# First attention: the causal triangle selected in SBUF by GpSimd, late exponentials, and products three steps behind the scores

## The chip, the cores and the metric

The kernel runs on one NeuronCore of one Trainium2 chip, in one launch. The metric is the device time in microseconds, as the median of several executions. A core has five engines that work side by side, each through its own queue in order: TensorE (PE), VectorE (DVE), ScalarE (ACT), GpSimd (POOL), and SyncE (SP), which here only issues transfers. They wait for each other through semaphores.

## The reference

The reference is a block of four parts over x of 1024 tokens by 512 channels: an attention of 32 heads of 16 channels, a mixture of low-rank experts, a second attention of 32 heads of 128 channels, and the experts again. The change lies in the first attention alone:

```python
x = x + _L0_attn_a_ref(_layernorm(x, axis=-1), wq, wk, wv, wo)

# inside, with hd = 16
scores = jnp.einsum('bqhd,bkhd->bhqk', xq, xk) * scale
causal = jnp.tril(jnp.ones((T, T), dtype=bool))
scores = jnp.where(causal[None, None], scores, NEG_INF)
probs = jax.nn.softmax(scores, axis=-1)
out = jnp.einsum('bhqk,bkhd->bqhd', probs, xv).reshape(B, T, C)
return out @ wo.T
```

Token q may only look at tokens k up to q. Everything is float32.

## The kernel before

`attention_a` first projects (`project_a`), then attends (`attend_a`). The 32 heads, each padded to 32 rows, make eight *chunks* `c` of four heads. Every chunk is computed twice over: once with queries on the partitions (*rows*, `row_scores` L358) to find each query's maximum, and once with keys on the partitions (*columns*, `col_scores` L407), where the maximum has been put into a spare channel of q, so that the scores come out with the maximum already taken off. The exponentials of the columns (`exponentials` L429) are then directly the left side of the product with v (`product` L449). One spare column of v holds ones, so the product also gives the sums of the softmax.

A chunk is cut into nine *steps* `n`, lists of pieces that make up to 512 score columns a head. In chunks 0 to 6 the columns go through `down_cols`: steps 0 to 3 are full blocks, step 4 is the diagonal of the second half of the queries (`qc` 1), 5 is beside it, 6 holds its rest and the first piece of `qc` 0, 7 is the diagonal of `qc` 0, and 8 its rest. Chunk 7 goes through `up_cols`, which begins with the diagonal of `qc` 0.

`step(rc, cc, n)` (L534) works on the rows of chunk `rc = cc + 1` and the columns of chunk `cc` at once, in two halves of two heads each. A half records: four score tiles on PE (two of columns, two of rows, each in a PSUM bank of `ps_s`, which has seven), the maxima on DVE (`maxima` L375, L378), the two exponentials on ACT, then whatever is due, then half of the product of an earlier step. `pending` holds the steps whose product is still to come; before the change a step's product is recorded two steps later (`len(pending) > 2`, L541).

In the diagonal steps 4 and 7, `exponentials` has the triangle added on PE: for each head four bfloat16 matmuls with the identity `identb` and `maskT` (L427) add -2^100 above the diagonal to the scores that are already in the bank, and the exponential then gives zero there.

`later` is a list of recorded work with a count; `due()` (L526) runs once in each half, lowers every count and records what has fallen below zero. It carries the end of a chunk. When the last product of a (chunk, qc) is recorded, `normalize` (L482) copies the sums and results out of the one PSUM bank of `ps_o` on ACT (L486), has SP move them (L493, L495), and puts two pieces into `later`: `invert` after 3 halves (the reciprocal L498 on DVE, transfers L500 and four of L502 that spread the inverses into `over`), and `multiply` after 8 (L508 on POOL, which needs the transfers of L495 and L502). Before the change `normalize` of `qc` 1 is reached in the first half of step 8 of its own chunk, and that of `qc` 0 in the second half of step 1 of the next. For chunks 6 and 7 `normalize_turned` (L468) does this with transposes on DVE. `with_maxima` (L389) transposes the maxima of the next chunk and has SP write them into q by four transfers (L397), at the end of steps 6 and 8.

The order in which instructions stand in each engine's queue is not that of the recording: a scheduler in the Tile layer orders them by its own estimate of when each could run. Instructions given to `keep_in_program_order` (the reciprocal L498 among them) keep their recorded order on their engine. Semaphore waits follow from what each instruction reads and writes. The tiles `p` of the exponentials come from the pool `a_pt` with five buffers of four heads by 512.

## Time and profile before

| what | value |
|---|---|
| median of 3 runs | 1570.44 us (1569.54 to 1571.32) |
| the profiled execution | 1571.58 us, its span 1569.8 us |
| busy share of the span: PE, DVE, ACT, POOL | 98%, 67%, 42%, 29% |
| mean granted PE clock | 0.999 |
| exponentials of the columns (L429) | 292 of 0.417 to 0.680 us, from 120.6 to 370.4 us |
| mask matmuls (L427) | 256 of 0.38 us, from 132.3 to 365.1 us |
| product matmuls (L449) | 1552, from 125.5 to 371.2 us |
| copies out of PSUM (L486) | 12 of 0.593 us, from 148.7 to 322.0 us |
| reciprocals (L498) | 12 of 0.533 us, from 155.9 to 329.2 us |
| multiplies on POOL (L508) | 12 of 1.272 us, from 165.2 to 338.7 us |

The span is the time from the first to the last instruction of one profiled execution; the execution's own time is 1.8 us longer. A row of a group gives the line, engine, operation, what it writes and reads, its shape and count, then its busy time in us and the mean in ns of one, and last the idle time of the engine just before such instructions and what ended it ("<-"). A row of a timeline gives the start, the length, the engine ("SPq" is SP's queue of transfers, whose length is that of issuing), the line and what ran, with the idle time before it and its releaser in brackets. Several instructions that follow each other without a gap are drawn as one row with their number, so a row of 1.08 us with "x2" is a pair of exponentials. A row of a stretch gives its bounds, its length, the busy time and number of instructions of PE, weight loads, DVE, ACT and POOL, the granted clock of PE as a share of the full one, and the share and rate of the transfers. A matmul's end is modelled, so a busy PE is not one at its peak.

### The profile page before, as it was taken

To read this page: it belongs to the slowest core of one execution; us is meant where nothing else is said; L and a number is where in the kernel's file an instruction comes from. 1 tells how busy PE (TensorE), PEld (TensorE's weight loads), DVE (VectorE), ACT (ScalarE), POOL (GpSimd) and SP (SyncE) were. 2 spreads that over 40 slices of the span, in tenths; PEclk is the share of its full clock that TensorE was granted. 3 is DMA by queue.
4 is the path that set the end of the run, shared out by engine and by line. 5 is a ranking of instruction groups with operands and counts; after the bars stand their busy time and mean duration, and the time that the engine had idled before them with its cause. 6 is when DMAs were issued, how large, how long until landed. Compare 5 with 4: busy or idle time off the path is not lost.

```text
span 1569.8 us, 32216 instructions
## 1 busy us (share of the span) xinstructions
PE 1543.4 (98%) x12894; PEld 926.1 (59%) x12894; DVE 1058.7 (67%) x2537; ACT 662.1 (42%) x1597; POOL 463.1 (29%) x571
## 2 busy tenths in 40 slices
PE   9999999999999999999999999999999999999998
PEld 5545455555555657557656755755765675556654
DVE  4557778773566886666776667766676766776753
ACT  2216666665223544443434444343343444433430
POOL 3000000002233433432443343334244333333450
PEclk9999999999999999999999999999999999999999
DMA  5000222220033102412330331241133032135001
GB/s 208 1 1 6 20 22 19 18 20 19 29 99 95 42 1 68 68 42 55 63 60 28 82 38 31 65 72 41 54 62 61 28 69 35 34 86 122 4 2 54
DMA packets 80950, 75.34 MB, mean 48 GB/s; under 512 B 14944, under 2 KB 56672, under 8 KB 80800
## 3 DMA queue, kind: packets, MB, share of 16 engines
q1 hardware_dynamic: 70272, 52.56, 14.3%
q0 software_dynamic: 8848, 17.58, 7.7%
q10 hardware_dynamic: 1680, 3.15, 0.5%
q8 instruction: 101, 1.65, 0.5%
q14 instruction: 49, 0.40, 0.1%
HBM read 33.08 MB, written 18.87 MB: 33 GB/s over the span
## 4 chain that ended last, share of the span: by engine, by line
PE 84%; DVE 7%; POOL 4%; ACT 2%; issue 2%; SPq 0%; DMA 0%; DVEq 0%; ACTq 0%; POOLq 0%
PE s L1079 13%; PE wo L765 12%; PE o L1140 11%; PE sT L407 8%; PE pq L993 8%; PE kv L920 5%; PE oT L449 5%; PE pm_f L714 3%; PE or L1140 3%; PE s L358 3%; PE pj_v L218 2%; PE pj_q L218 2%; PE pm_ao L1370 2%; PE pj_k L218 2%; DVE p L1081 2%
## 5 line engine op out<-in xcount | busy, mean ns | idle before, releaser
L1091 POOL TENSOR_SCALAR p<-p,rs 128x1024 f32<-128x1024 f32 (+7 forms) x256 | 192.8, 754 | 407.0 <-DVE rs L1090 406.3
L1079 PE MATMUL s<-kT,qT 128*128 128x512 f32 (+3 forms) x768 | 297.0, 496 | 10.9 <-DVE p L1081 10.9
L1079 PEld LDWEIGHTS s<-kT,qT 128*128 128x128 f32 x768 | 137.9, 190 | 174.7 <-issue 114.4
L765 PE MATMUL wo<-wo,oT 128*128 128x512 f32 x512 | 237.9, 593 | 1.0 <-ACT spare L781 1.0
L1106 DVE STREAM_TRANSPOSE pT<-p 128x512 f32<-128x512 f32 (+3 forms) x256 | 152.9, 602 | 109.5 <-PE o L1140 58.8
L1088 ACT ACTIVATE p<-p,nm 128x1024 f32<-128x1024 f32 (+7 forms) x256 | 198.3, 775 | 17.9 <-ACT nm L1086 0.4
L429 ACT ACTIVATE p<-sT 128x512 f32<-128x512 f32 (+1 forms) x292 | 155.2, 593 | 89.8 <-PE s L358 35.2
L1085 DVE TENSOR_REDUCE nm<-p 128x1 f32<-128x1024 f32 (+7 forms) x256 | 188.2, 735 | 2.9
L1140 PEld LDWEIGHTS o<-pT,va 32*128 32x128 f32 x4212 | 172.9, 185 | 21.7 <-issue 10.4
L1086 ACT ACTIVATE nm<-nm 128x1 f32<-128x1 f32 x256 | 51.6, 202 | 315.6 <-DVE nm L1085 314.7
L1140 PE MATMUL o<-pT,va 32*128 32x224 f32 (+5 forms) x4212 | 181.3, 324 | 0.8 <-DVE pT L1106 0.8
L358 PE MATMUL s<-kT,qT 32*128 32x512 f32 (+3 forms) x768 | 164.4, 520 | 0.0
L407 PE MATMUL sT<-qT,kT 32*128 32x128 f32 (+3 forms) x1152 | 155.3, 401 | 0.3 <-DMA qT<-negT 0.3
L765 PEld LDWEIGHTS wo<-wo,oT 128*128 128x128 f32 x512 | 94.2, 190 | 90.7 <-issue 78.8
L1081 DVE SCALAR_TENSOR_TENSOR p<-s,rq,relr 128x512 f32<-128x512 f32 x192 | 120.9, 646 | 9.9 <-PE s L1079 9.7
L993 PE MATMUL pq<-xnTb,wq 128*128 128x512 f32 x240 | 117.8, 600 | 0.4
L1081 DVE SCALAR_TENSOR_TENSOR p<-s,rq,rel 128x512 f32<-128x512 f32 (+1 forms) x192 | 102.5, 558 | 21.0 <-PE s L1079 20.9
L407 PEld LDWEIGHTS sT<-qT,kT 32*128 32x128 f32 x1152 | 80.6, 184 | 50.6 <-issue 29.4
L1112 DVE STREAM_TRANSPOSE tT<-p 128x512 f32<-128x512 f32 (+3 forms) x128 | 63.7, 498 | 57.0 <-POOL p L1091 30.6
L375 DVE TENSOR_REDUCE part<-s 128x1 f32<-128x512 f32 x128 | 81.6, 684 | 28.1 <-PE s L358 20.1
L1090 DVE RECIPROCAL rs<-ss 128x1 f32<-128x1 f32 x256 | 39.8, 155 | 85.9 <-ACT p L1088 82.1
L508 POOL TENSOR_TENSOR o<-o,over 64x512 f32<-64x512 f32 x12 | 15.3, 1272 | 270.1 <-DMA o<-oTs 224.0
(201 smaller groups left out, 2161.8 us busy)
## 6 DMA issues: line engine op xcount, KB each, us to landing
va<-v SPq DMA_DIRECT2D x256, 64.0 KB
xd<-beside POOLq DMA_DIRECT2D x56, 256.0 KB, 4.1
wq<-in_b_WqT_dram SPq DMA_DIRECT2D x8, 1024.0 KB
wo<-in_b_WoT_dram SPq DMA_DIRECT2D x8, 1024.0 KB
x_x<-in_x_dram SPq DMA_DIRECT2D x8, 256.0 KB
wkv<-in_b_WkT_dram SPq DMA_DIRECT2D x8, 256.0 KB
xd<-x_x ACTq DMA_DIRECT2D x8, 256.0 KB
wkv<-in_b_WvT_dram SPq DMA_DIRECT2D x8, 256.0 KB
```

Source lines behind the costliest of these rows:

```text
L358: nc.tensor.matmul(made[j][:, at:end], lhsT=qT[rows_of(j), c, i * P : (i + 1) * P], rhs=kT[rows_of(j), c, kc * QC : kc * QC + end - at], s ...
L407: nc.tensor.matmul(made[j][:, at:end], lhsT=kT[rows_of(j), c, b * P : (b + 1) * P], rhs=qT[rows_of(j), c, qc * QC + x0 : qc * QC + x1], st ...
L429: nc.scalar.activation(p[:, j, :end], made[j][:, :end], AF.Exp)
L765: nc.tensor.matmul(ps, lhsT=oTs[g, h][:, t * P : (t + 1) * P], rhs=wo[:, h, :], start=(h == heads[0]), stop=(h == heads[-1]))
L993: ins = nc.tensor.matmul(ps, lhsT=w[:, kc, :], rhs=x[:, kc, :], start=first and kc == 0, stop=kc == H - 1, skip_group_check=True,)
L1079: nc.tensor.matmul(s, lhsT=qT[:, i * P : (i + 1) * P], rhs=kT[:, lo:hi], start=True, stop=True)
L1081: nc.vector.scalar_tensor_tensor(p[:, lo:hi], s, rq[:, i : i + 1], rels[i % 2][:, at + lo : at + hi], ALU.mult, ALU.add)
L1085: nc.vector.tensor_reduce(nm, p[:, :w], AX.X, ALU.max, negate=True)
L1088: nc.scalar.activation(p[:, :w], p[:, :w], AF.Exp, bias=nm, scale=slope, accum_out=ss)
L1091: nc.gpsimd.tensor_scalar(p[:, :w], p[:, :w], rs, 1.0, ALU.mult, ALU.mult)
L1106: nc.vector.transpose(PT[:, i : i + (NT - 1) * (m - 1) + 1 : NT - 1, :], p[:, : m * P].rearrange("p (j k) -> p j k", k=P))
L1140: nc.tensor.matmul(cols(o[:, a], j, j + skip), lhsT=vs[g][j // 4][rows, j % 4 * NB + b, :], rhs=moving(j, j + skip, rows, slice(b * B, (b ...
```

## The change

In all chunks but the last the triangle is no longer added to the scores on PE. ACT writes `Relu(-s)` of the diagonal's scores s into `p` in SBUF; with the maximum taken off, a score on or below the diagonal is zero or negative, so this is -s there. POOL then sets what lies above the diagonal to 2^100 (`affine_select`, one instruction for the two heads of a half), and ACT takes `Exp(-p)` in place. That last exponential is put into `later`, head by head, with the counts 2, 3, 1 and 2 for heads 0 to 3: one falls due in each of the second half of the diagonal step, the two halves of the next step, and the first half of the one after. Since p is complete only then, the product of a step is recorded three steps behind its scores instead of two; at the first step of the last chunk two products are recorded, so that from there on the distance is two again.

```diff
             def col_scores(c, n, heads, made):
 
                 pieces = col_pieces(c, n)
-                masked = pieces[0][:4] in diagonal(pieces[0][0])
+                masked = c == NCA - 1 and pieces[0][:4] in diagonal(pieces[0][0])
...
+            def negated(of):
+                tc.keep_in_program_order(nc.scalar.activation(of, of, AF.Exp, scale=-1.0))
+
             def exponentials(c, n, heads, made, p):
                 pieces = col_pieces(c, n)
                 end = pieces[-1][-1]
 
-                if pieces[0][:4] in diagonal(pieces[0][0]):
+                masked = pieces[0][:4] in diagonal(pieces[0][0])
+                if masked and c == NCA - 1:
                     mask = maskT.unsqueeze(1).to_broadcast([P, len(pieces), P])
...
                             nc.tensor.matmul(to, lhsT=identb[:, rows], rhs=mask, start=False, stop=True)
+                if not masked or c == NCA - 1:
+                    for j in heads:
+                        nc.scalar.activation(p[:, j, :end], made[j][:, :end], AF.Exp)
+                    return
+
+
                 for j in heads:
-                    nc.scalar.activation(p[:, j, :end], made[j][:, :end], AF.Exp)
+                    nc.scalar.activation(p[:, j, :], made[j], AF.Relu, scale=-1.0)
+                lo, hi = min(heads), max(heads) + 1
+                of = p[:, lo:hi, :].rearrange("p j (a k) -> p (j a) k", k=P)
+                nc.gpsimd.affine_select(
+                    out=of,
+                    in_=of,
+                    compare_op=ALU.is_ge,
+                    fill=-NEG,
+                    base=0,
+                    pattern=[[0, (hi - lo) * (QC // P)], [1, P]],
+                    channel_multiplier=-1,
+                )
+                for j in heads:
+                    of = p[:, j, :]
+                    later.append([(2, 3, 1, 2)[j], lambda of=of: negated(of)])
...
-                turns = product(*pending.pop(0)) if len(pending) > 2 else iter(())
+                turns = iter(())
+                while len(pending) > (2 if cc in (None, NCA - 1) else 3):
+                    turns = chain(turns, product(*pending.pop(0)))
```

`chain` is that of `itertools`.

More of the change, by code (lines that the diff above doesn't have):

```diff
@@ L2 @@
 from contextlib import ExitStack
+from itertools import chain
 import concourse.bass as bass
```

## The prediction

> **What bounds the kernel now.** I read the page first, then the stretch from 120 to 372 us in which chunks 0 to 7 of the first attention run, because only there does the change act. TensorE sets the pace:

> ```profile
> 213.88:246.67 32.79, 32.79 (x469) 17.47 (x472) 26.39 (x84) 20.49 (x38) 2.54 (x2) 1.00 0.28 20
> 246.67:279.53 32.86, 32.86 (x468) 17.46 (x472) 26.39 (x84) 20.50 (x38) 2.54 (x2) 1.00 0.24 19
> 279.53:312.40 32.87, 32.87 (x469) 17.46 (x472) 26.38 (x84) 20.49 (x38) 2.54 (x2) 1.00 0.28 20
> ```

> These are the busy times in three stretches of one chunk each (after the length: PE, weight loads, DVE, ACT, POOL, then granted clock). PE is busy throughout, DVE 80%, ACT 62%, POOL nearly free. A chunk lasts 32.84 us. I call its nine steps 0 to 8 and a step's halves a and b; steps 4 and 7 hold the diagonal. The groups that the change touches:

> ```profile
> L429 ACT ACTIVATE p<-sT 128x512 f32<-128x512 f32 x270 | 145.5, 597 | 87.4 <-PE s L358 33.6 <-PE sT L427 32.5 <-PE sT L407 21.0
> L427 PE MATMUL sT<-maskT,identb 128*32 128x512 bf16 x256 | 19.3, 384 | 0.0
> ```

> ACT's timeline shows the rhythm: each row is a half's pair of exponentials, here steps 2a, 2b, 3a, 3b, 4a, 4b, 5a of one chunk:

> ```profile
> 224.44 1.08 ACT L429 ACTIVATE p<-sT 128x512 f32<-128x512 f32 x2 [0.35 <-PE s L358]
> 226.02 1.08 ACT L429 ACTIVATE p<-sT 128x512 f32<-128x512 f32 x2 [0.49 <-PE sT L407]
> 227.93 1.08 ACT L429 ACTIVATE p<-sT 128x512 f32<-128x512 f32 x2 [0.82 <-PE s L358]
> 229.51 1.09 ACT L429 ACTIVATE p<-sT 128x512 f32<-128x512 f32 x2 [0.49 <-PE sT L407]
> 231.81 1.09 ACT L429 ACTIVATE p<-sT 128x512 f32<-128x512 f32 x2 [1.21 <-PE sT L427]
> 233.84 1.08 ACT L429 ACTIVATE p<-sT 128x512 f32<-128x512 f32 x2 [0.94 <-PE sT L427]
> 235.59 1.08 ACT L429 ACTIVATE p<-sT 128x512 f32<-128x512 f32 x2 [0.67 <-PE s L358]
> ```

> A plain step takes 227.93 - 224.44 = 3.49 us, its halves 1.58 and 1.91. In 4a and 4b the pair waits for L427, the mask products. Last, the chain that scales a finished chunk: SP issues L500 after the reciprocal, then L502, and POOL's multiply waits for these to land.

> ```profile
> 222.74 0.66 SPq L500 DMA_DIRECT2D over<-sums  x1
> 224.75 2.46 SPq L502 DMA_DIRECT2D over<-over  x4
> ```

> ```profile
> 231.71 1.27 POOL L508 TENSOR_TENSOR o<-o,over 64x512 f32<-64x512 f32 x1 [22.90 <-DMA o<-oTs]
> ```

> The first fence is SP's timeline, the second POOL's. From L500's start to the multiply it is 231.71 - 222.74 = 8.97 us; in the six chunks 8.7 to 9.0, mean 8.85. The profile names an older transfer as releaser, but the distance from L502's start hardly varies (6.7 to 7.0 us), so it is this one. POOL sits idle meanwhile, and today that costs nothing.

> **Removed: the mask products.** 16 matmuls in each of 14 diagonal steps. Seven plain steps take 7 x 3.49 = 24.43 of the 32.84 us, so a diagonal step takes 4.20, 0.71 more than a plain one: 14 x 0.71 = 9.9 us. That is what they cost net of the short wait that they cover in other steps. The gross bound is 0.44 us from one group of eight to the products behind it, 28 x 0.44 = 12.3. I take -9.9, as it is read on the path.

> **Added on ACT.** The pair in a diagonal half becomes a Relu of the same shape and source (0.54 each, as now), and four exponentials follow later, one behind the pair in each of halves 4b, 5a, 5b, 6a (and 7b, 8a, 8b, next 0a). A half then holds 3 x 0.54 = 1.62 us of ACT against a half of 1.58 to 1.91: it fits, with at most 0.04 late in the short halves. Shapes in SBUF (L1088, 128x512) show 722 ns with a bias and an accumulator; at that price a half would hold 1.80 and 28 short halves lose up to 0.2 each, 5.6 us. I take 0, because the pitch of L429 is what back-to-back work shows, and keep part of this for the upper end. A change of activation table (1.28 us in its single row of this page) could not be borne 56 times, but the changed program as built loads a table once, as now.

> One place has no room. In 0a the late exponential now stands ahead of the copy of the finished sums (L486), which moves there from 8a. The copy starts 1.08 + 0.54 = 1.62 us behind the pair instead of 0.97, and the next products and the pair of 0b both wait for it: 0.6 us, in six chunks +3.6 us (0 if a later wait absorbs it).

> **Added on POOL: 28 selects of 128x1024.** No row has this size. The select of 128x512 takes 742 ns, that of 128x128 282: 1.198 ns an element, so 1.36 us. A dearer row, L151's tensor_scalar of 128x512 with two pointers, takes 2086 ns, or 4.2 us for 1024. I take 1.36, the same operation. Alone it would be hidden: the Relus of 4a end 1.08 us into the half, the select some 1.4 us later, and the first late exponential is due only behind the pair of 4b.

> **Moved: products and what hangs on them, by one step.** This decides. The finished sums of qc 1 are copied in 0a instead of 8a, the inversion falls in 2a instead of 1a, and so L500, the L502 group and the landing all come 3.49 us later. POOL's queue as built holds, in each of chunks 1 to 6: the multiply of the previous chunk's qc 1, *then* the two selects of step 4, then the multiply of qc 0, then the two selects of step 7. The scheduler put the multiply where it guessed the landing. The select behind it cannot start first, and behind that select wait, in ACT's queue, one late exponential and every pair after it.

> In the chunk shown: L500 started 1.79 us after the pair of 1a (220.95). After 2a's pair that is 224.44 + 1.79 = 226.23; landing 8.97 later, 235.20. Without masks the Relus of 4a run 229.51 + 1.91 = 231.42 to 232.50 and those of 4b 233.00 to 234.08; then ACT needs the select of 4a. It gets it at 235.20 + 1.27 (multiply) + 1.36 (select) + 0.1 = 237.9. The late exponential ends at 238.5 and 5a's pair, due at 233.00 + 1.91 = 234.91, starts 3.6 us late. With the mean of 8.85 it is 3.5. TensorE cannot run ahead: there are seven score banks and four are filled per half, and in 5b the fourth tile takes the bank that 5a's first exponential frees. So TensorE stands still for about 3.3 us and the whole 3.5 us is on the path: 6 x 3.5 = +21.0 us. The multiply of qc 0 comes 3.5 us later too, but the stall has then moved 7a back by as much, and its selects find POOL free: 0. SP's queue loses no order that matters; the transfers of the next maxima now go ahead of the copy's, which delays the latter under 1 us, and the sums still land before 2a.

> **The ends.** At the passage to chunk 7 a product of 1.14 us is made up, the transposes of `normalize_turned` fall where TensorE has nothing between (1.0 instead of 0.59), and one late exponential stands behind four (0.4); chunk 0 starts 0.9 us lighter. Together +1.0.

> **The clock.** A standing TensorE can lose its clock:

> ```profile
> 555.00:560.00 5.00, 3.24 (x18) 1.55 (x16) 4.76 (x11) 3.09 (x7) 2.12 (x3) 1.00 0.00 0
> 560.00:565.00 5.00, 5.00 (x18) 2.48 (x11) 2.75 (x10) 3.02 (x8) 2.21 (x2) 0.66 0.00 0
> ```

> After 1.76 us without PE work the granted clock was 0.66 over the next 5 us, 1.7 us lost. Another idle time of 1.87 us (490 to 500) left it at 1.00. So six stalls cost between 0 and 6 x 1.5 = 9.0 (0.2 each hidden in waits); I take the half that one in two gives, +4.5. [...]

> **Sum.** -9.9 + 3.6 + 21.0 + 1.0 + 4.5 = +20.2. On the profiled execution, 1571.58 + 20.2 = 1591.8 (span 1569.8 + 20.2 = 1590.0); the median shown is 1.14 lower, so 1590.6: I predict 1590. Its own range: from -12.3 with copies 0, clock 0 and landings 0.25 us earlier (-1.5), +8.2 or 1579, to clock +9.0 and late exponentials +4, +28.7 or 1599.

> **Rivals.**
> 1. *The transfers land before the selects want POOL.* Then the masks are simply saved: -9.9 + 3.6 + 1.0 = -5.3, 1565. It needs the multiply to start by 234.1 - 0.1 - 1.36 - 1.27 = 231.4, 3.8 us before my 235.2. Against it speak six landings within 0.3 us of each other; for it, that the transfers of the maxima no longer stand between. Chance 0.11.
> 2. *The stall is short*, around 1.5 us, since the chain partly runs closer in its new place: -9.9 + 9 + 3.6 + 1.0 = +3.7, with the gross saving of 12.3 about +1: 1571 to 1574. Chance 0.08.
> 3. *Selects are dear* (4.2 us by L151): 2.8 us more in each of 6 stalls, and in the other 8 diagonal steps the first late exponential waits about 2.6: +20.2 + 17 + 21 = 1628. The same operation's own rows speak against it. With 2 us a select it is some 1601. Chance 0.08.
> 4. *The change does nothing*: excluded, as the built program has the 28 selects and 224 matmuls fewer.

> **Numbers.** My case has 0.73. The range 1574 to 1600 takes in the upper part of rival 2 and the lower of rival 3. A difference of 0.2% (3.1 us) is about what a measurement of this kernel can tell from none; rivals 1 and 2 give faster 0.12 and same 0.05, the rest is slower, 0.83.

> **What would show it.** Right: multiplies on POOL in step 4 with a select directly behind them, ACT idle some 3.5 us on POOL in 4b of chunks 1 to 6 and not in chunk 0, PE idle on ACT in 5b, chunk 0 at 31.4 us and the next ones about 36, a granted clock under 1 in some. Wrong: step 4 selects ahead of the multiply's landing, ACT waiting for no select, all chunks near 31.5 us; or waits on POOL in step 7 as long as in step 4, which would make the select itself the cause.

## The result, and the profile after

The changed kernel takes 1592.81 us in the median of 5 runs (1585.27 to 1595.45), the kernel before 1570.44 beside it (5 runs, 1569.54 to 1572.22). The ratio is 1.0132, with a 95% interval of 1.0103 to 1.0161: slower, by 20.7 us (by the two medians 22.4). The profiled execution is the quickest of those runs, 1585.27 us (span 1583.5, clock 0.997); the other four had 0.989 to 0.991. Two more executions on record took 1585.41 us at 0.997 and 1594.71 us at 0.989. That spread in time goes with the clock: span times clock is 1578.7 us for the profiled run and 1575.3 to 1576.7 for the four others.

ACT's timeline shows the place. These are 2a and 2b, then 3b to 5a, of one middle chunk:

```profile
227.02 1.09 ACT L435 ACTIVATE p<-sT 128x512 f32<-128x512 f32 x2 [0.70 <-PE s L359]
228.66 1.08 ACT L435 ACTIVATE p<-sT 128x512 f32<-128x512 f32 x2 [0.56 <-PE sT L408]
...
232.10 1.08 ACT L435 ACTIVATE p<-sT 128x512 f32<-128x512 f32 x2 [0.49 <-PE sT L408]
234.15 1.08 ACT L440 ACTIVATE p<-sT 128x512 f32<-128x512 f32 x2 [0.96 <-PE sT L408]
236.03 1.09 ACT L440 ACTIVATE p<-sT 128x512 f32<-128x512 f32 x2 [0.80 <-PE s L359]
240.42 0.63 ACT L418 ACTIVATE p<-p 128x512 f32<-128x512 f32 x1 [3.30 <-POOL p L443]
240.96 1.06 ACT L435 ACTIVATE p<-sT 128x512 f32<-128x512 f32 x2
```

L440 is the Relu of 4a and 4b, L418 the late exponential, L435 the plain pair of 5a. The Relus of 4a were done at 235.23 and those of 4b at 237.12, yet ACT then stood idle for 3.30 us until L443, the select of 4a, had come. The six middle chunks show such a wait of 2.88, 3.01, 3.30, 3.09, 3.29 and 3.00 us, 18.6 in all; chunk 0 shows none.

POOL's timeline tells why, first chunk 0, then the same middle chunk:

```profile
132.67 1.09 POOL L443 TENSOR_SCALAR_AFFINE_SELECT p<-p 128x1024 f32<-128x1024 f32 x1 [78.06 <-ACT p L440]
...
238.08 1.26 POOL L533 TENSOR_TENSOR o<-o,over 64x512 f32<-64x512 f32 x1 [21.07 <-DMA o<-oTs]
239.30 2.14 POOL L443 TENSOR_SCALAR_AFFINE_SELECT p<-p 128x1024 f32<-128x1024 f32 x2
```

In chunk 0 the select follows its own Relu. In the middle chunk POOL idles 21.07 us in front of the multiply L533, and both selects run back to back behind it ("x2"), the first 4 us after its data was ready. SP's timeline gives the other end of that chain:

```profile
228.87 0.70 SPq L525 DMA_DIRECT2D over<-sums  x1
230.91 2.43 SPq L527 DMA_DIRECT2D over<-over  x4
```

From the issue at 228.87, 1.85 us after the pair of 2a, to the multiply at 238.08 are 9.21 us. TensorE's timeline, and below it two neighbouring stretches of 5 us, show what became of the wait:

```profile
241.59 0.58 PE L359 MATMUL s<-kT,qT 32*128 32x384 f32 x1 [2.61 <-ACT p L435]
```

```profile
310.00:315.00 5.00, 2.41 (x28) 1.18 (x26) 1.77 (x9) 3.13 (x7) 2.88 (x3) 0.96 0.44 18
315.00:320.00 5.00, 5.00 (x58) 2.60 (x58) 3.29 (x17) 3.20 (x7) 1.27 (x1) 0.70 0.32 11
```

The score matmul of 5b waits for the bank that 5a's exponential frees. The two stretches belong to a later chunk with the same wait: TensorE, busy 2.41 of 5 us, then works at a granted clock of 0.70. The groups of the new instructions, by form over the first attention:

```profile
L418 ACT ACTIVATE p<-p 128x512 f32<-128x512 f32 x56 | 35.4, 633 | 19.5 <-POOL p L443 19.5
...
L443 POOL TENSOR_SCALAR_AFFINE_SELECT p<-p 128x1024 f32<-128x1024 f32 x28 | 30.2, 1090 | 99.8 <-ACT p L440 91.9 <-DVE neg L379 7.6
```

A select takes 1.09 us, and all idle time ahead of the late exponentials is put down to POOL. The table sets the periods of a chunk side by side, from one chunk's transfers of the maxima to the next one's (L397 before, L398 after).

| | before | after |
|---|---|---|
| chunk period, us | 32.84, 33.36, 32.78, 32.86, 32.88 | 36.13, 34.74, 36.65, 34.82, 36.58 |
| ACT waits for the select, us | none | six of 2.88 to 3.30, one of 0.89 at the end |
| clock of the profiled run | 0.999 | 0.997 |

The long and short periods after alternate. The granted clock explains it: in this execution it fell after the stalls at 170, 241 and 313 us (to 0.66, 0.67 and 0.70 in the next 5 us or so) and stayed at 1.00 after those at 206 and 278. The three chunks with the fall have a mean of 36.45 us, the two without 34.78: a lost clock cost 1.7 us.

Finer stretches show which stalls cost the clock in this execution. The rows come in pairs, for the first three stalls: a stretch with the stall or half of it, and the stretch after it.

```profile
167.80:171.20 3.40, 1.22 (x13) 0.68 (x10) 0.62 (x4) 2.11 (x4) 2.31 (x3) 1.00 0.13 13
171.20:174.60 3.40, 3.40 (x30) 1.63 (x32) 1.81 (x9) 1.75 (x5) 0.00 (x0) 0.51 0.89 28
205.40:208.80 3.40, 2.28 (x30) 1.48 (x34) 1.28 (x5) 3.39 (x7) 0.97 (x1) 1.00 0.55 21
208.80:212.20 3.40, 3.40 (x58) 1.91 (x52) 3.22 (x19) 2.97 (x6) 0.00 (x0) 1.00 0.56 21
239.50:242.90 3.40, 1.31 (x16) 0.84 (x18) 0.31 (x1) 2.47 (x5) 1.94 (x2) 1.00 0.48 18
242.90:246.30 3.40, 3.40 (x32) 1.43 (x24) 2.10 (x11) 1.99 (x5) 0.00 (x0) 0.50 0.63 21
```

### The profile page after: what moved, and what is told of

Its sections match the earlier page's. It is cut to its first block, busy times and chain, and to the rows that moved or that the text cites. A ratio compares the mean times of both kernels' runs of the same rounds, so it can differ in the third digit from the quotient of the medians.

```text
span 1583.5 us, 31835 instructions
## 1 busy us (share of the span) xinstructions
PE 1543.1 (97%) x12670; PEld 923.0 (58%) x12670; DVE 1058.2 (67%) x2537; ACT 689.7 (44%) x1653; POOL 493.0 (31%) x599
## 3 DMA queue, kind: packets, MB, share of 16 engines
q8 instruction: 99, 1.62, 0.4%
## 4 chain that ended last, share of the span: by engine, by line
PE 77%; DVE 8%; POOL 4%; ACT 4%; issue 3%; DMA 2%; SPq 2%; DVEq 0%; ACTq 0%; POOLq 0%
PE s L1106 13%; PE wo L792 12%; PE o L1167 11%; PE pq L1020 7%; PE sT L408 5%; PE kv L947 5%; PE oT L474 4%; PE pm_f L741 3%; PE or L1167 3%; PE s L359 2%; PE pj_v L219 2%; PE pj_q L219 2%; PE pm_ao L1397 2%; PE pj_k L219 2%; DVE p L1108 2%
## 5 line engine op out<-in xcount | busy, mean ns | idle before, releaser
L359 PE MATMUL s<-kT,qT 32*128 32x512 f32 (+3 forms) x768 | 173.5, 530 | 12.5 <-ACT p L435 12.5
L408 PE MATMUL sT<-qT,kT 32*128 32x128 f32 (+3 forms) x1152 | 162.4, 410 | 0.0
L435 ACT ACTIVATE p<-sT 128x512 f32<-128x512 f32 (+1 forms) x236 | 125.0, 594 | 34.6 <-PE s L359 20.1
L474 PE MATMUL oT<-p,v_p 128*32 128x128 f32 (+1 forms) x1552 | 91.5, 337 | 2.3 <-ACT oTs L511 2.1
```

The lines of the kernel that those rows point to most:

```text
L359: nc.tensor.matmul(made[j][:, at:end], lhsT=qT[rows_of(j), c, i * P : (i + 1) * P], rhs=kT[rows_of(j), c, kc * QC : kc * QC + end - at], s ...
L408: nc.tensor.matmul(made[j][:, at:end], lhsT=kT[rows_of(j), c, b * P : (b + 1) * P], rhs=qT[rows_of(j), c, qc * QC + x0 : qc * QC + x1], st ...
L474: nc.tensor.matmul(o[rows_of(j), x0 + p0 - at : x0 + p1 - at], lhsT=v_cols(b, c * HC + j), rhs=p[:, j, p0:p1], start=first, stop=last,)
```

## The experiments

Times are medians, ratios are against the kernel before on the same chip, with 95% intervals. Diffs are against the changed kernel unless something else is said.

**1. The order in POOL's queue put right.** Since the scheduler places the multiply by its own estimate, both instructions are kept in program order, and the multiply is recorded one half later, behind the selects of step 4.

```diff
-                nc.gpsimd.affine_select(
+                select = nc.gpsimd.affine_select(
...
+                tc.keep_in_program_order(select)
...
-                    nc.gpsimd.tensor_tensor(to, to, over[at : at + HC * DA, :], ALU.mult)
+                    tc.keep_in_program_order(nc.gpsimd.tensor_tensor(to, to, over[at : at + HC * DA, :], ALU.mult))
...
-                later.append([8, multiply])
+                later.append([9, multiply])
```

> The changed kernel with POOL's selects and multiplies kept in recorded order and the multiply recorded after 9 halves instead of 8, so that both selects of a diagonal step stand ahead of the multiply that falls into it. Theory (the multiply, waiting for its transfers, holds back the selects behind it): the waits of the late exponentials on POOL fall from 19.5 us to under 3 us in all, the granted clock stays at 0.999, and the time is 1565 us (1561 to 1569): the masks saved (-9.9), the late copies (+3.6) and the ends (+1.0) remain. Rival (the select and the late exponentials themselves are too slow for ACT): waits and time stay as in the changed kernel, 1583 to 1595 us. Second rival (the distance of three steps costs by itself): 1575 us or more.

Measured: 1562.21 us (1562.18 to 1562.29), ratio 0.9947 (0.9933 to 0.9962), clock 1.0. POOL's timeline in this kernel, then ACT's:

```profile
227.32 1.09 POOL L443 TENSOR_SCALAR_AFFINE_SELECT p<-p 128x1024 f32<-128x1024 f32 x1 [16.98 <-ACT p L440]
229.15 1.09 POOL L443 TENSOR_SCALAR_AFFINE_SELECT p<-p 128x1024 f32<-128x1024 f32 x1 [0.73 <-ACT p L440]
230.21 1.27 POOL L534 TENSOR_TENSOR o<-o,over 64x512 f32<-64x512 f32 x1
```

```profile
227.99 1.09 ACT L440 ACTIVATE p<-sT 128x512 f32<-128x512 f32 x2 [0.80 <-PE s L359]
228.97 0.63 ACT L418 ACTIVATE p<-p 128x512 f32<-128x512 f32 x1
229.51 1.09 ACT L435 ACTIVATE p<-sT 128x512 f32<-128x512 f32 x2
```

The multiply now stands behind both selects and finds its transfers landed. The late exponential follows the Relus of 4b with no idle time, and 5a's pair starts 1.52 us after 4b's instead of 4.93. The selects, the late exponentials and the third step are all still in this kernel, so the loss came from the order on POOL; with it put right, the change gains 0.5%.

**2. One late exponential moved out of the copy's way.** Experiment 1, and head 1's late exponential one half later, so that it no longer stands ahead of the copy in 0a.

```diff
-                    later.append([(2, 3, 1, 2)[j], lambda of=of: negated(of)])
+                    later.append([(2, 4, 1, 2)[j], lambda of=of: negated(of)])
```

> As e1_order, and the late exponential of head 1 one half later (count 4 instead of 3), so that in step 0a the copy of the finished sums stands directly behind the pair. Theory (a late exponential ahead of the copy delays products and the next pair by 0.6 us in six chunks): 3 to 4 us below e1_order, 1561 to 1562 us. Rival (that delay is absorbed by a later wait): within 1 us of e1_order.

Measured: 1560.05 us (1559.26 to 1561.39), ratio 0.9934 (0.9920 to 0.9949). It is 2.2 us below experiment 1, and the best version of this study, below both kernels.

**3. The inversion one half earlier.** This moves the landing and nothing of the selects.

```diff
-                later.append([3, invert])
+                later.append([2, invert])
```

> The changed kernel with the inversion after 2 halves instead of 3, POOL's order unchanged: the transfers land one half (1.6 to 1.9 us) earlier. Theory: each of six waits of ACT on POOL shrinks from about 3.1 to about 1.4 us, 10 us together, and stalls of some 1.3 us of TensorE seldom cost the clock: 1570 to 1576 us. Rival (select or late exponentials too slow): no change, 1583 to 1595 us.

Measured: 1571.35 us (10 runs, 1569.72 to 1573.99), ratio 1.0008 (0.9998 to 1.0017), clock 0.998 to 1.0. ACT's waits in the middle chunks fell to 1.38, 1.21, 1.38, 1.32, 1.41 and 2.06 us, and POOL's timeline still has the multiply in front:

```profile
231.28 1.26 POOL L533 TENSOR_TENSOR o<-o,over 64x512 f32<-64x512 f32 x1 [19.14 <-DMA o<-oTs]
232.51 2.13 POOL L443 TENSOR_SCALAR_AFFINE_SELECT p<-p 128x1024 f32<-128x1024 f32 x2
```

With the same wrong order and an earlier landing the loss against the kernel before is gone; what is left against experiment 1, (1.0008 - 0.9947) x 1570.4 = 9.6 us, is about the sum of the six waits, 8.8. What sets the length of the stall is when the transfers land. The clock's loss went with it, though waits of 1.2 to 2.1 us were left.

**4. The inversion one half later.** The opposite step, `later.append([4, invert])`.

> The changed kernel with the inversion after 4 halves instead of 3, POOL's order unchanged: the transfers land one half (1.6 to 1.9 us) later. Theory: six waits of ACT on POOL of about 4.8 instead of 3.1 us, 10 us more; with all stalls of TensorE near 4.5 us the clock falls in every chunk: 1600 to 1606 us, granted clock 0.988 to 0.991. Rival (the stall is bounded by something else than the landing, such as the banks or the maxima): within 4 us of the changed kernel.

Measured: 1617.04 us (1615.71 to 1618.29), ratio 1.0292 (1.0278 to 1.0306), clock 0.982: more than the theory gave, in its direction. The waits of this kernel, and two of its stretches:

```profile
ACT p L418 <- POOL p L443: 35.3, 6, 6.2
```

```profile
250.00:255.00 5.00, 0.40 (x7) 0.40 (x8) 0.45 (x2) 1.56 (x4) 3.35 (x3) 0.67 0.26 16
255.00:260.00 5.00, 5.00 (x38) 2.41 (x38) 1.94 (x9) 2.43 (x6) 0.84 (x1) 0.50 0.54 17
```

The six waits sum to 35.3 us, 16.7 more than in the changed kernel. After 5 us in which TensorE was busy for 0.40, the next 5 us run at a granted clock of 0.50. Span times clock is 1584.8 us, 29 us less than the span. That is 17 falls of 1.71 us: at five of the six stalls the half clock lasted 10.2 us, three of the falls seen above in a row, and at the last 6.8. Of these 58 us at half the clock some 15 lie within the stalls themselves, where they cost nothing, so the clock's share of the time is nearer to 22 us than to 29. The waits grew by 2.8 us each, more than a half lasts. In the chunk of these stretches it was 2.3, as L525, now behind a transfer of the next sums in SP's queue, was issued 3.93 us after the pair of 2a instead of 1.85; the others were not traced.

**5. What the masks were worth.** The kernel before with the mask products left out in chunks 0 to 6 and nothing put in their place: the causal triangle is missing there, and the exponentials of the diagonal steps are scaled down so that they stay finite.

```diff
-                masked = pieces[0][:4] in diagonal(pieces[0][0])
+                masked = c == NCA - 1 and pieces[0][:4] in diagonal(pieces[0][0])
...
-                if pieces[0][:4] in diagonal(pieces[0][0]):
+                triangle = pieces[0][:4] in diagonal(pieces[0][0])
+                if triangle and c == NCA - 1:
...
-                    nc.scalar.activation(p[:, j, :end], made[j][:, :end], AF.Exp)
+                    nc.scalar.activation(p[:, j, :end], made[j][:, :end], AF.Exp, scale=2.0**-8 if triangle and c < NCA - 1 else 1.0)
```

(against the kernel before)

> The kernel before with the mask products left out in chunks 0 to 6, so the causal triangle is missing there (the exponential of those steps is scaled by 2^-8, to keep it finite); nothing is put in their place. It measures the saving alone. By a diagonal step against a plain one: 9.9 us, 1560.5 us. By the gross time of the products on TensorE: 12.3 us, 1558 us. If other engines bound the diagonal steps as soon as the masks are gone: under 5 us, above 1565 us.

Measured: 1562.62 us (1562.14 to 1563.85), ratio 0.9951 (0.9936 to 0.9966), which is (1 - 0.9951) x 1570.4 = 7.7 us. ACT's timeline, 3b to 5a:

```profile
225.69 1.08 ACT L430 ACTIVATE p<-sT 128x512 f32<-128x512 f32 x2 [0.49 <-PE sT L407]
227.80 1.09 ACT L430 ACTIVATE p<-sT 128x512 f32<-128x512 f32 x2 [1.02 <-PE sT L407]
229.83 1.08 ACT L430 ACTIVATE p<-sT 128x512 f32<-128x512 f32 x2 [0.95 <-PE s L358]
231.41 1.08 ACT L430 ACTIVATE p<-sT 128x512 f32<-128x512 f32 x2 [0.49 <-PE s L358]
```

These distances are 2.11, 2.03 and 1.58 us; before they were 2.30, 2.03 and 1.75. Without masks a diagonal step is still not a plain one: 4b waits as long as it did, only for another matmul. Step 4 gains 0.36 us here, step 7 of the same chunk 0.61.

**6. Three steps alone.** The kernel before, with products three steps behind the scores and the masks as they were.

```diff
-                turns = product(*pending.pop(0)) if len(pending) > 2 else iter(())
+                turns = iter(())
+                while len(pending) > (2 if cc in (None, NCA - 1) else 3):
+                    turns = chain(turns, product(*pending.pop(0)))
```

(against the kernel before)

> The kernel before with its products three steps behind the scores and nothing else changed: masks on TensorE, no selects, no late exponentials. e1_order gained 7.8 us and e4_masks_left_out only 7.4, though e1_order also carries late exponentials that cost it 2.2 us at the copies, so some 2.6 us came from elsewhere. Theory: from the distance of three itself (the copy of the sums no longer stands ahead of SP's transfers of the maxima, and the transposes at the passage to the last chunk move): 1567 to 1568 us. Rival (the prediction's +1.0 for the ends, the rest being other savings of taking the masks off TensorE): 1570 to 1572 us. POOL waits as long for the transfers as in the changed kernel, and that costs nothing here: no PE stall, clock 0.999 or more.

Measured: 1570.01 us (11 runs) beside 1570.99 (21 runs) of the kernel before, ratio 0.9990 (0.9981 to 0.9999). The distance costs nothing by itself; by the ratio it gains 1.6 us, with an interval of 0.2 to 3.0, by the medians 1.0. The theory's 2.6 us are not borne out. In the profile 1.1 us of the gain lie in the five middle periods, 32.71 to 32.73 us here against 32.78 to 33.36.

**7. Two steps again, with the right order.** Experiment 1 with `while len(pending) > 2`.

> e1_order with products two steps behind the scores again, all else equal. Theory (the third step is what makes room for the late exponentials): the first half of a product in 6a and 0a now needs head 1's late exponential, recorded in the same half, so TensorE waits about 1.3 us in 14 steps: 1575 to 1582 us. Rival (three steps were not needed): 1560 to 1565 us.

Measured: 1586.33 us (1585.71 to 1588.12), ratio 1.0099 (1.0083 to 1.0114), clock 1.0: 24 us above experiment 1, more than expected. The waits of this kernel name it:

```profile
PEld oT L475 <- ACT p L418: 22.7, 27, 1.4
```

The weight loads of the products wait 27 times for late exponentials. The third step, which moves the whole closing chain later, is what makes the deferral affordable with the late exponentials where they are. Earlier ones were not tried with two steps.

**8. Each select done twice.** Experiment 1 with the select issued two times over.

```diff
-                select = nc.gpsimd.affine_select(
+                for _ in range(2):
+                  select = nc.gpsimd.affine_select(
```

> e1_order with each select issued twice (the second changes nothing), so that POOL takes 2.18 us where it took 1.09. Theory (the select alone is hidden, with about 0.5 us to spare behind the pair of the next half): the first late exponential waits 0.4 to 0.7 us in 14 steps, 6 to 9 us above e1_order, 1568 to 1571 us. If the select were what the changed kernel waited for, e1_order would already show waits, and here 14 x 1.09 = 15 us more, 1577 us.

Measured: 1569.98 us (1569.38 to 1572.49), ratio 0.9997 (0.9987 to 1.0006): 7.8 us above experiment 1. The late exponential in 4b and 7b now waits for POOL, in each of the 14 diagonal steps, by 0.36 to 0.59 us, 7.2 in all. So the single select of 1.09 us is hidden with 0.5 to 0.7 us to spare, and a select of twice the price costs all of the gain.

**9 and 10. TensorE kept at work while it waits.** In 5b of chunks 1 to 6 the changed kernel gets additional matmuls in front of the one that stands still. They change no result, as a real matmul overwrites theirs. In the first version that is the score matmul before it, done eight times instead of once; in the second, 14 products of the identity with the mask.

```diff
+                        fill = x == 0 and n == 5 and j == 1 and 0 < c < NCA - 1
+                        for z in range(8 if fill else 1):
                           nc.tensor.matmul(
...
-                            stop=x == len(pieces) - 1 and not masked,
+                            stop=x == len(pieces) - 1 and not masked or fill and z < 7,
```

> The changed kernel, with the last score matmul that TensorE can run before it stands still (128x384, of one head, in 5b of chunks 1 to 6) done eight times instead of once into the same tile. The stall of ACT on the select stays as it is (waits of ACT on POOL near 3.3 us, six times); only TensorE's idle time of 2.6 to 3.3 us is filled, with matmuls that use 32 of the 128 rows. Theory (the clock is lost because TensorE stands still): the span times the granted clock of the changed kernel's runs is 1575 to 1579 us, so with the clock at 0.999 to 1.0 the time is 1577 to 1582. Rival (the clock falls for another reason, or matmuls of 32 rows do not hold it): the clock stays near 0.991 and the time at 1588 to 1596.

```diff
+                        fill = x == 0 and n == 5 and j == 1 and 0 < c < NCA - 1
+                        for _ in range(14 if fill else 0):
+                            to = made[j][:, at:end].rearrange("p (a k) -> p a k", k=P)
+                            mask = maskT.unsqueeze(1).to_broadcast([P, (end - at) // P, P])
+                            nc.tensor.matmul(to, lhsT=identb, rhs=mask, start=True, stop=True)
```

> The same filling at the same place by 14 bfloat16 products of the identity and the mask, 128x384 each, which use all 128 rows and columns, ahead of the real score matmul that overwrites them. Theory (idle time alone costs the clock): clock 0.999 to 1.0 and 1577 to 1583 us, like the filling with scores; if only matmuls of all rows hold the clock, this run alone shows 1.0. Rival (another cause): 1588 to 1596 at 0.991.

Measured: with scores 1600.61 us (1598.87 to 1602.26), ratio 1.0183 (1.0168 to 1.0198), clock 0.990 to 0.993; with full rows 1581.13 us (1580.69 to 1582.63), ratio 1.0062 (1.0045 to 1.0079), clock 0.999 to 1.0. The kernel before had 1571.83 on this chip. Two stretches around the first stall, of the filling with scores:

```profile
165.00:170.00 5.00, 5.00 (x42) 2.93 (x39) 2.83 (x13) 2.05 (x5) 3.35 (x3) 1.00 0.13 34
170.00:175.00 5.00, 5.00 (x25) 2.67 (x23) 1.10 (x5) 2.05 (x5) 0.00 (x0) 0.55 0.75 26
```

and of the filling with full rows:

```profile
165.00:170.00 5.00, 5.00 (x50) 2.54 (x42) 2.92 (x13) 2.12 (x5) 3.36 (x3) 1.00 0.15 34
170.00:175.00 5.00, 5.00 (x69) 2.78 (x68) 3.72 (x19) 4.59 (x9) 0.00 (x0) 1.00 0.76 30
```

PE is busy for all 5 us in all four rows. With one head's score matmuls the clock fell to 0.55; with matmuls on all 128 rows it stayed at 1.00. ACT's waits on the select sum to 17.9 and 18.0 us over six, much as in the changed kernel. So the second version removes the clock's loss alone, and the first speaks against the simple theory that idle time alone costs the clock: to be busy in the profile was not enough. The two fillings differ in the rows used (32 and 128) and in the type (float32 and bfloat16), and which of the two decides was not tried. Span times clock of the first is 1584.2 us, about 7 above the changed kernel, so there the filling also overran the stall. Its clock fell at all six stalls, for 6.8 us at the first and for 3.4 us at the third and the fourth.

## Why the prediction was right, and where its terms were off

The forecast of 1590 us stood against 1592.81, and by the mechanism that it named. Its terms, measured apart:

| term | predicted, us | measured, us | from |
|---|---|---|---|
| masks saved | -9.9 | -7.7 | experiment 5 |
| late exponential ahead of the copy | +3.6 | +2.0 | experiment 2 against 1 |
| ends | +1.0 | not apart; the distance of three as a whole -1.6 | experiment 6 |
| these three together | -5.3 | -8.3 | experiment 1 |
| six stalls | +21.0 | +18.1 | experiment 10 against 1 |
| clock | +4.5 | +11.0 | after against experiment 10 |
| sum | +20.2 | +20.7 | ratio 1.0132 |

All are worked out from the ratios, as the chips differ: (1.0062 - 0.9947) x 1570.4 = 18.1 for the stalls and (1.0132 - 1.0062) x 1570.4 = 11.0 for the clock, the others in the same way. By the intervals of the ratios each is uncertain by some 1 to 5 us. The last three rows above the sum lead step by step from the kernel before over experiments 1 and 10 to the changed one, so that they add up is no test. The three small ones add up to -7.3; the 1.0 us that is missing to -8.3 is within the intervals and was not traced.

- **The queue on POOL: right.** The multiply stood ahead of the selects of step 4 in chunks 1 to 6, ACT waited 2.88 to 3.30 us in 4b, TensorE 2.2 to 2.6 us in five of the 5b's (0.39 in the last). Step 7 had no wait but the 0.89 us of chunk 6. Experiments 1, 3 and 4 turn the stall off, down and up by its two handles, the order and the landing.
- **The dates: right.** L525 was issued 1.85 us after the pair of 2a, predicted 1.79; to the multiply it took 9.21 us, predicted 8.85 to 8.97.
- **The stall's size: somewhat too large.** A select took 1.09 us and not 1.36. That is 0.27 in each stall, 1.6 of the 2.9 us; the rest, 0.2 a stall, was not traced. Scaling by elements from 128x128 and 128x512 overstated 128x1024. The periods say the same without the ratios: the two chunks with a stall and no fall of the clock last 34.74 and 34.82 us, those of experiment 1 31.67 to 31.70, so a stall is 3.1 us long.
- **Saving too large.** The step priced a diagonal step without masks at a plain step's 3.49 us. Experiment 5 shows that without them about half of step 4's extra time stays: it gained 0.36 us and step 7 0.61, where 0.71 had been reckoned for each. For the ends nothing was measured apart. The prediction had no term for a gain of the third step in the middle chunks, where experiment 6 shows one; with the ends, as far as that kernel has them, it comes out 2.6 us lower than reckoned.
- **The clock too small.** 11.0 us, uncertain by some 5, stand against bounds of 0 to 9.0. The profiled run alone, at 0.997, would have borne out 4.5: it lost its clock after three of the five long stalls, 5.1 us. The four others lost more, (1 - 0.991) x 1591 = 14 us by the clock at the median. They took 7 to 10 us longer than the profiled run, which at 1.7 us each is four to six falls more than its three. Where those fell was not traced, nor whether all lay in the first attention; experiments 4 and 9 show that one stall can cost more than one fall. The idle times of the profiled run were 2.18, 2.31, 2.61, 2.39 and 2.59 us, and the clock was lost after the first, third and fifth and kept after the second and fourth. So the length of the idle time alone doesn't decide it; in all five what lies within one stretch of the estimated raster separates the lost (1.85 to 2.18 us) from the kept (at most 1.16 and 1.45). That is not the whole of it either: the prediction's idle time of 1.87 us kept its clock at 1.00, and experiment 9 lost it (0.55) with TensorE busy.

That the sum came out within 3 us is thus partly luck: the clock's 6.5 us too little were made up by 2.9 us too much for the stalls and 3.0 too much for the three small terms together. Among the rivals, the first (transfers land before the selects want POOL, 1565) is what experiment 1 produces by order instead, 1562; the second (a short stall, 1571 to 1574) is what experiment 3 produces, 1571. The third (dear selects) falls with the 1.09 us, though experiment 8 shows how close it stood.

## What to carry to other kernels

Before giving an idle engine new work that is due soon, look at what stands in its queue and what each piece waits for: in the kernel before, POOL stood idle for 22.90 us in front of the multiply while TensorE was busy for all 32.79 us of that chunk, since nothing urgent stood behind it. In the changed kernel the scheduler, which orders by estimated times, put the urgent selects behind; pin the order of the two, as in experiment 1 (1562.21 us against 1592.81). And a stall of the pacing engine should be priced twice, once in its length and once in the clock afterwards (here 18.1 and 11.0 us), over several runs and not one profile.

## What the runs showed of the hardware

- A TensorE that was busy in the profile lost its clock in one filling and not in the other: with 32x384 float32 matmuls of a single head the granted clock fell to 0.55 in the 5 us after (experiment 9), with 128x384 bfloat16 ones it stayed 1.00 (experiment 10).
- In the profiled run of the changed kernel, idle times of TensorE of 2.18, 2.61 and 2.59 us were followed by a fall of the clock, and those of 2.31 and 2.39 us were not. In experiment 4, 5 us with 0.40 us of TensorE's work were followed by 5 us at 0.50.
- The falls in the changed kernel lasted 3.41 us each at 0.50, 1.71 us lost in each; in experiment 4 the half clock lasted 10.2 us at five stalls and 6.8 at one. The starts lay whole multiples of 3.41 us apart: 71.7 in the changed kernel (21 times), 41.0 from the first stall to the second in experiment 4 (12), 78.5 from the first to the third and 75.1 from there to the fifth in experiment 9 (23 and 22).
- GpSimd's select over 128x1024 float32 took 1.09 us in the changed kernel, less than in proportion to the 0.742 us of 128x512 in the kernel before.
- ScalarE's exponential from SBUF to SBUF (L418) took 0.633 us for a 128x512 in the changed kernel, not much more than the 0.599 us of one from PSUM (L435).
